# A two-group kernel with masked weights: results on another queue, masks among leaves, weight builds moved, a looser order

## The chip, the cores and the metric

The kernel runs on one core of a Trainium2 chip. The metric is the device time of one execution in microseconds (us). A core has TensorE (matrix products), VectorE and ScalarE (elementwise work), GpSimd, and SyncE, which here only issues transfers. Each engine runs its own instructions in one fixed order and waits where data, a buffer or a transfer isn't there yet. Transfers (DMAs) are issued by SyncE, ScalarE or GpSimd, and sixteen DMA engines carry them out.

## The reference

There are 8 batches of 256 tokens with 1024 features. The first layer adds, for each batch, a matrix product whose weights depend on the batch: a shared W0 plus a matrix of signs, +1 or -1 from a 0/1 mask of integers (1024 x 1024 per batch), scaled by the batch's coefficient. The second layer is a linear layer shared by all batches, plus a low-rank adapter (LoRA) of rank 16 picked for each batch.

```python
def _L0_cond_ref(hidden_states, W, b, coeff, mask):
    output = jnp.einsum('bsi,oi->bso', hidden_states, W) + b
    sign = (2 * mask - 1).astype(hidden_states.dtype)
    diff = jnp.einsum('bsi,bio->bso', hidden_states, sign)
    return output + diff * coeff[:, None, None]

def _L1_cond_ref(x, adapter_mapping, W, b, lora_As, lora_Bs):
    base_out = jnp.einsum('bti,oi->bto', x, W) + b
    A = lora_As[adapter_mapping]
    Bm = lora_Bs[adapter_mapping]
    lora_h = jnp.einsum('bti,bir->btr', x, A)
    lora_out = jnp.einsum('btr,bro->bto', lora_h, Bm)
    return base_out + lora_out * SCALING

x = x + _L0_cond_ref(x, L0_cond_W, L0_cond_b, condB_coeff, mask)
x = x + _L1_cond_ref(x, itok, L1_cond_W, L1_cond_b, lora_As, lora_Bs)
```

All data is float32, the masks are int32. A mask of one batch is 4 MB, all masks 32 MB.

## The kernel before, in words

**Two groups of four batches.** Each group runs the first layer of its four batches and then one second layer for all four: batches 0 to 3, second layer of group 0, batches 4 to 7, second layer of group 1. Everything is held transposed, features on the partitions.

**Pieces.** The effective weights of a batch are made in eight pieces of 128 x 1024 (`pieces`, lines 141 and 142); pieces 32 to 39 are those of batch 4. `load` (L173) issues a piece's mask (512 KB, L206), and for each of a batch's first four pieces also a tile of its tokens x (256 KB, L210), all on SyncE's queue. `build` (L222) turns the mask in place into weights in two steps: a conversion on ScalarE (L237, mask times 2c minus c) and an addition of W0 on VectorE (L245). The buffers of batch 4's first six pieces come from a pool of six ("w"), which the second layer of group 0 also uses for sums; the last two pieces, the second layer's results and the weight sums of batch 4 share a pool of ten ("q").

**First layer of batches 3 to 7 (`Seven`).** The 2 x 2 block product is done with seven products in place of eight (Strassen in Winograd's form). `operands` (L375) yields 20 steps a batch: eight pieces, the weight sums s1 to s4 in two halves each (L356, VectorE) and the token sums t1 to t4 (L373, VectorE). `products` (L447) issues seven products in 14 halves of 16 matmuls (L419). Results are read with the bias by ScalarE (`with_bias`, L438) or added by VectorE (`add`, L443). `Sevens.run_one` (L511) makes operands 10 steps ahead of the halves.

**Second layer (`second_layer`, L692).** Two levels of the same scheme. The outer level has seven products, `plan = ["A11", "A12", "S1", "S2", "S4", "S3", "A22"]`, run 0 to run 6. Each is again seven inner products of eight matmuls (L714) with seven weight tiles, the leaves a11, s1, s2, a12, s3, a22, s4 (256 KB each). The leaves are computed once, during group 0, and written to memory by GpSimd's queue (`keep`, L527, L531). `load_leaves` (L701, L704) reads the seven leaves of the next product into a pool of seven buffers, on SyncE's queue; it is called in the middle of each run (L815), so a leaf goes out when an older one has been used. `begin` (L762) starts the next product's a11 before the present product is finished. `read` (L766) takes results out of TensorE's banks: VectorE adds where there is something to add to, and ScalarE copies otherwise. `store` (L773) sends a finished 256 KB block of the output.

**What fills the second layer of group 0.** `next_masks(n)` (L871) issues loads of batch 4's first n pieces, and `next_weights(n)` (L877) makes the first n operand steps of batch 4 (their first four are the pieces 32 to 35). Both do nothing in group 1. A generator handed to `run` as `beside` gives a step at each of four places inside the run and what is left of it at its end. In the last run, `finish` (L830) gives the rest out between its last products.

**The order on the engines.** The tile framework plans each engine's order ahead, from the order in which the program names the instructions and from its own durations. `with behind(name)` (L144) adds an edge: the instructions in the block stand, on their own engine, after the instruction last kept under that name in `anchors`. So `behind("leaves")` puts masks after the last leaf issued, `behind("bias")` puts conversions after the last bias, `behind("adds")` puts additions of weights after the last sum, `behind("reads")` after the last read of the second layer.

Of the kernel before, what the change touches and what calls it, by code (L numbers as in the profile page):

```python
# [16 lines left out]
CG = 2  # L17
# [7 lines left out]
def kernel(  # L25
# [38 lines left out]
    nc = tc.nc  # L64
# [7 lines left out]
    NGROUP = B // GB  # L72
# [64 lines left out]
    anchors = {}  # L137
# [6 lines left out]
    def behind(what: str):  # L144
        return tc.issue_after(anchors[what].ins) if what in anchors else nullcontext()
# [104 lines left out]
    def load_to(n: int):  # L250
        nonlocal loaded
        while loaded < min(n, n_pieces):
            load(loaded)
            loaded += 1
# [5 lines left out]
    def bank(name):  # L260
        return psum.tile([P, 2, T], F32, tag="ps", name=name)
# [67 lines left out]
    class Seven:  # L329
# [105 lines left out]
        def with_bias(self, i, v, ps):  # L435
            for j in range(TPH):
                ot = i * TPH + j
                anchors["bias"] = nc.scalar.activation(  # L438
                    self.out(i, v)[:, j, :], ps[:, j, :], AF.Identity, bias=b0_sb[:, ot : ot + 1]
                )  # L440

        def add(self, i, v, ps):
            anchors["weights"] = anchors["adds"] = nc.vector.tensor_add(  # L443
                self.out(i, v), ps, self.out(i, v)
            )

        def products(self):  # L447

# [243 lines left out]
    def second_layer(group: int, y, first, first_steps, second):  # L692
# [6 lines left out]
        left_leaf, right = {}, {}  # L699

        def load_leaves(name):  # L701
            for n in ("a11", "s1", "s2", "a12", "s3", "a22", "s4"):
                t = lpool.tile([P, CG, OQ], F32, tag="l", name=f"l{group}_{name}_{n}")
                anchors["leaves"] = nc.sync.dma_start(t, leaf_at[name, n])  # L704
                left_leaf[name, n] = t
# [56 lines left out]
        def begin(n, name, r):  # L762
            banks[n] = bank(f"X_{group}_{n}")
            product(banks[n], left_leaf[name, "a11"], r.b[0, 0], first=True)

        def read(out, ps, other=None):  # L766
            if other is None:
                anchors["copies"] = nc.scalar.copy(out, ps)  # L768
                return anchors["copies"]
            own["reads"] = anchors["reads"] = nc.vector.tensor_add(out, ps, other)  # L770
            return anchors["reads"]

        def store(o, i, j, u, v, c=slice(0, CG), queue=nc.scalar):  # L773
            queue.dma_start(outT[GB * group + 2 * j + v, 2 * i + u][:, c], o)

        UV = [(0, 0), (0, 1), (1, 1), (1, 0)]
# [1 line left out]
        def run(n, name, r, seed, out, dest=None, beside=None, early=None, mid=None, late=None, then=None):  # L778

            leaf = {k: left_leaf.pop((name, k)) for k in ("a11", "s1", "s2", "a12", "s3", "a22", "s4")}
            other = seed or {uv: None for uv in UV}
            beside = beside or iter(())
            X = banks.pop(n)

            def done(uv):
                if dest:
                    store(out[uv], *dest, *uv)
                if then:  # L790
                    then(uv)

            read(out[0, 0], X, other[0, 0])
            Z = bank(f"Z_{group}_{n}")
            product(Z, leaf["s1"], r.t["t1"], first=True)
            if early:
                early()
            product(X, leaf["s2"], r.t["t2"])
            next(beside, None)
            read(out[0, 1], X, other[0, 1])  # L800
            Y = bank(f"Y_{group}_{n}")
            product(Y, leaf["a12"], r.b[1, 0], first=True)
            read(out[0, 0], Y, out[0, 0])
            done((0, 0))
            if mid:
                mid()
            if n + 1 == len(plan):
                finish(X, Z, leaf, r, other, out, dest, beside, done)
                return
            product(X, leaf["s3"], r.t["t3"])  # L810
            next(beside, None)
            read(out[1, 1], X, other[1, 1])
            read(out[1, 1], Z, out[1, 1])
            done((1, 1))
            load_leaves(plan[n + 1])  # L815
            begin(n + 1, plan[n + 1], right[plan[n + 1]])
            next(beside, None)
            product(X, leaf["a22"], r.t["t4"])
            read(out[1, 0], X, other[1, 0])
            done((1, 0))  # L820
            next(beside, None)
            if late:
                late()
            product(Z, leaf["s4"], r.b[1, 1])
            read(out[0, 1], Z, out[0, 1])
            done((0, 1))
            for _ in beside:
                pass

        def finish(X, Z, leaf, r, other, out, dest, beside, done):  # L830


            read(out[1, 1], Z, other[1, 1])
            product(X, leaf["s3"], r.t["t3"])
            next(beside, None)
            anchors["turn"] = read(out[1, 1], X, out[1, 1])
            done((1, 1))
            product(Z, leaf["s4"], r.b[1, 1])
            for _ in beside:
                pass  # L840
            read(out[0, 1], Z, out[0, 1])
            done((0, 1))
            product(X, leaf["a22"], r.t["t4"], by_tile=True)
            for c in range(CG):
                read(out[1, 0][:, c], X[:, c], other[1, 0][:, c])
                store(out[1, 0][:, c], *dest, 1, 0, c, (nc.sync, nc.scalar)[c])

        def quads(name):
            two = [pair(f"{name}{u}_{group}") for u in range(2)]
# [2 lines left out]
        def add(o, x):  # L852
            nc.vector.tensor_add(o, o, x)  # L853

        plan = ["A11", "A12", "S1", "S2", "S4", "S3", "A22"]
        right.update({"A11": first, "A12": second, "S4": Right(f"b22_{group}", b22)})
        big_t = {}

        def outer_sum(n, x, y, name):


            big_t[n] = [
                tpool.tile([P, TPH, T], F32, tag="T", name=f"T{n}_{group}_{v}") for v in range(2)
            ]
            right[name] = Right(f"T{n}_{group}", big_t[n])
            for v in range(2):
                nc.vector.tensor_sub(big_t[n][v], x[v], y[v])
                yield
            yield from right[name].sums()

        def next_masks(n):  # L871

            with behind("leaves"):
                if group + 1 < NGROUP:
                    load_to((group + 1) * GB * 2 * NG + n)

        def next_weights(n):  # L877
            if group + 1 < NGROUP:
                while sevens[group + 1].made < n:
                    sevens[group + 1].begin(sevens[group + 1].made + 1)  # L880
                    yield


        def ordered(steps):

            while True:
                with behind("reads" if "reads" in own else "layer"):
                    if next(steps, True):
                        return
                yield  # L890

        own = {}
        s3 = ordered(later["S3"] if group == 0 else iter(()))
# [3 lines left out]
        for _ in ordered(first_steps):  # L897
            pass
        t1 = ordered(outer_sum(1, b12, b11, "S1"))
        e1, c11, c12 = quads("e1"), quads("c11"), quads("c12")  # L900
# [3 lines left out]
            beside=chain(islice(s3, 1), ordered(second.sums()), islice(s3, 4), islice(t1, 2)),  # L904
            early=down,
            mid=lambda: up(0, 0, lower),
            late=lambda: up(0, 1, lower),
            then=lambda uv: add(c11[0, 0], e1[0, 0]) if uv == (1, 1) else None,
        )
        for uv in UV[1:]:  # L910
# [4 lines left out]
            dest=(0, 0),  # L915
            beside=chain(t1, s3, islice(t2, 2)),
        )
        next_masks(2)
        e5 = quads("e5")
        run(  # L920
            2, "S1", right["S1"], None, e5,
            beside=chain(t2, ordered(right["S4"].sums())),
            then=lambda uv: add(c12[uv], e5[uv]),
        )
        next_masks(4)
        run(
            3, "S2", right["S2"], e1, e1,
            beside=chain(ordered(outer_sum(3, b22, b12, "S3")), next_weights(2)),
            then=lambda uv: add(c12[uv], e1[uv]),
        )  # L930
        c21, c22 = quads("c21"), quads("c22")
# [1 line left out]
        run(  # L933
            4, "S4", right["S4"], c12, c12,
            dest=(0, 1),
            beside=chain(ordered(outer_sum(4, b21, big_t[2], "A22")), next_weights(3)),
            mid=lambda: up(1, 0, upper),
            late=lambda: up(1, 1, upper),
        )
# [1 line left out]
        def add_e5():  # L941

            for uv in UV:
                with behind("reads"):
                    add(c22[uv], e5[uv])
                yield

        run(5, "S3", right["S3"], e1, e1, beside=chain(add_e5(), next_weights(4)), then=lambda uv: add(c21[uv], e1[uv]))


        next_masks(6)
# [1 line left out]
        def last_quarter():  # L953
            for u, v in UV:
                add(c22[u, v], e1[u, v])
                store(c22[u, v], 1, 1, u, v)
                yield

        run(6, "A22", right["A22"], c21, c21, dest=(1, 0), beside=last_quarter())
        nonlocal limit  # L960
        limit = n_pieces

# [143 lines left out]
```

## Time and profile before

| | before |
|---|---|
| time, median of 3 runs | 418.19 us (417.73 to 419.43) |
| the profiled execution's own time | 420.21 us |
| its span, first to last instruction | 418.5 us |
| TensorE busy | 404.1 us (97%), 2554 matmuls, mean granted clock 0.992 |
| VectorE busy | 312.8 us (75%) |
| ScalarE busy | 136.4 us (33%) |
| GpSimd busy | 42.8 us (10%) |
| moved by DMA | 99.56 MB, 238 GB/s on average |

The stages of the span, read from TensorE's timeline: batches 0 to 3 until about 114.7 us, second layer of group 0 from 114.7 to 219.4, batches 4 to 7 from 219.4 to 320.8, second layer of group 1 from there to the end. Inside the first of the second layers, the runs begin their a11 at about 114.7 (A11), 128.4 (A12), 140.1 (S1), 159.5 (S2), 174.3 (S4), 190.5 (S3) and 203.9 us (A22).

How to read the lines: L714 is line 714 of the kernel; "X<-T,l_S_a" names what an instruction writes and reads, without buffer numbers; a note in brackets at the end of a line is the time that the engine stood idle before it and what ended it. PE is TensorE, PEld its weight load, DVE VectorE, ACT ScalarE, POOL GpSimd, SPq SyncE's queue. In tables of stretches the columns are the stretch, its length, the busy time (and number) of TensorE, its weight loads, VectorE, ScalarE and GpSimd, then TensorE's granted clock, the busy share of the DMA engines and GB/s. In tables of waits, the numbers are the time in all, how often, and the longest.

### The profile page before, as it was taken

How to read it: one execution, taken by the hardware profiler on the slowest of the kernel's cores; microseconds unless marked ns; L12 is line 12 of the kernel's file. 1: busy time of each engine (PE TensorE's matmuls, PEld its weight loads, DVE VectorE, ACT ScalarE, POOL GpSimd, SP SyncE). 2: the span in 40 equal slices, each digit the busy share in tenths (PEclk: the TensorE clock that was granted, in tenths of full speed). 3: DMA queues.
4: the chain of work that ended last, by engine and by line, in shares of the span. 5: the costliest groups of instructions: out<-in, count | busy, mean ns of one | idle time of the engine just before them, and what ended most of it. 6: DMA issues, size and time to landing. Idle time of an engine off the chain costs nothing.

```text
span 418.5 us, 6751 instructions
## 1 busy us (share of the span) xinstructions
PE 404.1 (97%) x2554; PEld 359.8 (86%) x2554; DVE 312.8 (75%) x446; ACT 136.4 (33%) x221; POOL 42.8 (10%) x85
## 2 busy tenths in 40 slices
PE   8999999999999977899999999999999999999996
PEld 6888888899968766678889999999999788888885
DVE  3357688999706883997899999899843177898593
ACT  4443625771034012303041844537421330101100
POOL 0000252009750120000000001300000000000000
PEclk9999999999999996999999999999999999999999
DMA  8999999961996795745699965904011337554644
GB/s 291 404 401 398 401 408 413 402 248 41 364 366 215 233 330 222 257 161 167 199 369 360 407 210 191 311 3 152 27 52 60 93 125 232 171 153 157 217 153 151
DMA packets 42404, 99.56 MB, mean 238 GB/s; under 512 B 5636, under 2 KB 6404, under 8 KB 42372
## 3 DMA queue, kind: packets, MB, share of 16 engines
q1 hardware_dynamic: 32690, 76.17, 52.0%
q0 software_dynamic: 4928, 14.71, 9.4%
q10 hardware_dynamic: 4754, 8.26, 5.4%
q8 instruction: 20, 0.33, 0.3%
q14 instruction: 12, 0.10, 0.1%
HBM read 79.19 MB, written 19.92 MB: 237 GB/s over the span
## 4 chain that ended last, share of the span: by engine, by line
PE 84%; DMA 9%; DVE 4%; SPq 1%; issue 1%; DVEq 0%
PE X L714 22%; PE X L419 15%; PE ps L278 13%; PE Z L714 10%; PE Z L419 8%; PE Y L714 5%; PE ps L303 4%; DMA l_S_a<-leaf_S_a 4%; PE Y L419 3%; PE G L732 2%; DMA x<-xT 2%; PE psh L749 2%; DMA w_sb<-w0T 2%; DVE w L245 1%; DMA w<-mask 1%; DMA l_S_s<-leaf_S_s 1%
## 5 line engine op out<-in xcount | busy, mean ns | idle before, releaser
L245 DVE TENSOR_TENSOR w<-w,w_sb 128x1024 f32<-128x1024 f32 (+1 forms) x67 | 77.4, 1172 | 27.3 <-ACT w L237 20.8
L237 ACT ACTIVATE w<-w,neg_c,two_c 128x1024 f32<-128x1024 int32 (+1 forms) x67 | 78.6, 1204 | 57.6 <-DMA w<-mask 46.9
L278 PE MATMUL ps<-x,w 128*128 128x256 f32 x256 | 55.4, 379 | 0.0
L278 PEld LDWEIGHTS ps<-x,w 128*128 128x128 f32 x256 | 48.6, 190 | 6.6
L853 DVE TENSOR_TENSOR c<-c,e 128x512 f32<-128x512 f32 x48 | 32.1, 683 | 11.3 <-ACT e L768 6.7
L438 ACT ACTIVATE y<-X,b_sb 128x128 f32<-128x128 f32 x60 | 17.1, 368 | 67.1 <-PE X L419 67.1
L419 PE MATMUL X<-t,s 128*128 128x128 f32 x288 | 34.1, 275 | 0.7 <-DVE s L356 0.7
L419 PEld LDWEIGHTS X<-t,s 128*128 128x128 f32 x288 | 33.0, 192 | 0.9 <-DVE s L356 0.9
L742 ACT COPY c<-G 128x512 f32<-128x512 f32 x32 | 16.5, 599 | 48.4 <-PE G L732 47.4
L303 PE MATMUL ps<-x,w 128*128 128x256 f32 x128 | 28.5, 384 | 0.3 <-DVE w L245 0.3
L303 PEld LDWEIGHTS ps<-x,w 128*128 128x128 f32 x128 | 24.6, 193 | 4.3 <-DVE w L245 0.9
L768 ACT COPY e<-X 128x512 f32<-128x512 f32 x16 | 9.4, 586 | 56.3 <-PE X L714 56.3
L770 DVE TENSOR_TENSOR e<-Y,e 128x512 f32<-128x512 f32 x8 | 5.5, 689 | 25.8 <-PE Y L714 14.0
L714 PE MATMUL X<-T_t,l_S_s 128*128 128x256 f32 x96 | 22.8, 380 | 1.0 <-DVE e L770 1.0
L770 DVE TENSOR_TENSOR c<-X,c 128x512 f32<-128x512 f32 (+1 forms) x26 | 16.6, 645 | 8.7 <-PE X L714 8.7
L419 PE MATMUL X<-t,w 128*128 128x128 f32 x192 | 22.5, 276 | 0.1
L419 PEld LDWEIGHTS X<-t,w 128*128 128x128 f32 x192 | 21.9, 192 | 0.3 <-DVE y L443 0.3
L356 DVE TENSOR_TENSOR s<-w,w 128x1024 f32<-128x1024 f32 x18 | 21.7, 1217 | 0.1
L714 PEld LDWEIGHTS X<-T_t,l_S_s 128*128 128x128 f32 x96 | 18.2, 190 | 3.9 <-DVE e L770 1.4
L419 PE MATMUL Z<-t,s 128*128 128x128 f32 x160 | 18.8, 275 | 0.0
L419 PE MATMUL Y<-x,w 128*128 128x128 f32 x160 | 18.7, 275 | 0.0
L419 PE MATMUL X<-x,w 128*128 128x128 f32 x160 | 18.7, 275 | 0.0
(144 smaller groups left out, 664.7 us busy)
## 6 DMA issues: line engine op xcount, KB each, us to landing
w<-mask SPq DMA_DIRECT2D x61, 512.0 KB, 7.1
l_S_s<-leaf_S_s SPq DMA_DIRECT2D x32, 256.0 KB, 2.7
x<-xT SPq DMA_DIRECT2D x31, 256.0 KB, 7.2
outT<-c ACTq DMA_DIRECT2D x30, 256.0 KB, 2.6
l_A_s<-leaf_A_s SPq DMA_DIRECT2D x24, 256.0 KB, 2.7
l_S_a<-leaf_S_a SPq DMA_DIRECT2D x24, 256.0 KB, 2.6
w<-w1T SPq DMA_DIRECT2D x16, 256.0 KB, 7.2
leaf_A_s<-A_s POOLq DMA_DIRECT2D x12, 256.0 KB, 6.6
```

The source lines that it names most:

```text
L237: nc.scalar.activation(w[:, i], m[:, i], AF.Identity, bias=neg_c[:, b : b + 1], scale=two_c[:, b : b + 1],)
L245: weff_at[k] = nc.vector.tensor_add(w[:, i], w[:, i], w0_of(k)[:, i])
L278: nc.tensor.matmul(ps[j // 2][:, j % 2, :], lhsT=w[:, c, j * P : (j + 1) * P], rhs=x_sb[b, g][:, c, :],  start=first and j % 2 == 0, stop= ...
L303: nc.tensor.matmul(ps[ot // 2][:, ot % 2, :], lhsT=w[:, h, j * P : (j + 1) * P], rhs=x_sb[0, c // CG][:, c % CG, :], start=c == 0 and ot % ...
L356: anchors["weights"] = op(s, self.w[x, a], self.w[y, a])
L419: anchors["products"] = nc.tensor.matmul(ps[:, j, :], lhsT=w[:, c, j * P : (j + 1) * P], rhs=r, start=first and a == 0 and c == 0 and j == ...
L438: anchors["bias"] = nc.scalar.activation(self.out(i, v)[:, j, :], ps[:, j, :], AF.Identity, bias=b0_sb[:, ot : ot + 1])
L714: anchors["inner"] = nc.tensor.matmul(ps[:, j, :], lhsT=l[:, c, j * P : (j + 1) * P], rhs=r[:, c, :], start=first and c == 0 and j == 0, s ...
L742: nc.scalar.copy(dest[b // 2][u, b % 2], ps[b])
L768: anchors["copies"] = nc.scalar.copy(out, ps)
L770: own["reads"] = anchors["reads"] = nc.vector.tensor_add(out, ps, other)
L853: nc.vector.tensor_add(o, o, x)
```

## The change

Four edits, all of them in how work is ordered or queued; what is computed stays.

- *Stores.* In group 0 all results go out on GpSimd's queue; before, ScalarE issued them, and SyncE one half of the last block. In group 1 the queues are as before.
- *Masks.* `next_masks(2)` and `next_masks(4)` ahead of runs 2 and 3 are gone. In their place `load_leaves` lets one more mask (with its x) out between the leaves a12 and s3, from product S1 on: piece 32 with S1, 33 with S2, 34 with S4, 35 with S3, 36 with A22. `next_masks(6)` ahead of run 6 stays.
- *Builds.* Operand steps 1 and 2 of batch 4 were made in run 3, step 3 in run 4, step 4 in run 5. Now steps 1 and 2 are made in run 5, and 3 and 4 in run 6.
- *Order.* The last bias of a batch, (1, 0), is no longer kept under "bias", and the sum (0, 1) no longer under "adds", so later conversions and additions needn't stand behind them.

```diff
         def with_bias(self, i, v, ps):
             for j in range(TPH):
                 ot = i * TPH + j
-                anchors["bias"] = nc.scalar.activation(
+                sent = nc.scalar.activation(
                     self.out(i, v)[:, j, :], ps[:, j, :], AF.Identity, bias=b0_sb[:, ot : ot + 1]
                 )
+            if (i, v) != (1, 0):
+                anchors["bias"] = sent
 
         def add(self, i, v, ps):
-            anchors["weights"] = anchors["adds"] = nc.vector.tensor_add(
-                self.out(i, v), ps, self.out(i, v)
-            )
+            anchors["weights"] = nc.vector.tensor_add(self.out(i, v), ps, self.out(i, v))
+            if i == v:
+                anchors["adds"] = anchors["weights"]
...
         def load_leaves(name):
             for n in ("a11", "s1", "s2", "a12", "s3", "a22", "s4"):
+                if n == "s3":
+                    next_masks(max(0, plan.index(name) - 1))
                 t = lpool.tile([P, CG, OQ], F32, tag="l", name=f"l{group}_{name}_{n}")
...
-        def store(o, i, j, u, v, c=slice(0, CG), queue=nc.scalar):
+        out_queues = (nc.gpsimd, nc.gpsimd) if group + 1 < NGROUP else (nc.scalar, nc.sync)
+
+        def store(o, i, j, u, v, c=slice(0, CG), queue=out_queues[0]):
             queue.dma_start(outT[GB * group + 2 * j + v, 2 * i + u][:, c], o)
...
-                store(out[1, 0][:, c], *dest, 1, 0, c, (nc.sync, nc.scalar)[c])
+                store(out[1, 0][:, c], *dest, 1, 0, c, out_queues[1 - c])
...
-        next_masks(2)
         e5 = quads("e5")
...
-        next_masks(4)
         run(
             3, "S2", right["S2"], e1, e1,
-            beside=chain(ordered(outer_sum(3, b22, b12, "S3")), next_weights(2)),
+            beside=ordered(outer_sum(3, b22, b12, "S3")),
...
         run(
             4, "S4", right["S4"], c12, c12,
             dest=(0, 1),
-            beside=chain(ordered(outer_sum(4, b21, big_t[2], "A22")), next_weights(3)),
+            beside=ordered(outer_sum(4, b21, big_t[2], "A22")),
...
-        run(5, "S3", right["S3"], e1, e1, beside=chain(add_e5(), next_weights(4)), then=lambda uv: add(c21[uv], e1[uv]))
+        run(5, "S3", right["S3"], e1, e1, beside=chain(add_e5(), next_weights(2)), then=lambda uv: add(c21[uv], e1[uv]))
...
-        run(6, "A22", right["A22"], c21, c21, dest=(1, 0), beside=last_quarter())
+        run(
+            6, "A22", right["A22"], c21, c21,
+            dest=(1, 0),
+            beside=chain(last_quarter(), next_weights(4)),
+        )
```

## The prediction

> **What bounds the kernel now.** I read the page's first two parts, the waits of TensorE, its timeline from 110 to 300 us, the SyncE queue and the chain of waits in the same stretch, and last the busy time of VectorE by stretches. TensorE is busy for 404.1 of 418.5 us; it starts at about 17 us, and nothing before 140 us is touched by the change. So what can be won is what TensorE loses later. Its waits, longest first, and its timeline in the first second layer:
>
> ```profile
> PE X L714 <- DMA l_S_a<-leaf_S_a: 5.4, 2, 4.7
> ```
>
> ```profile
> 152.96 1.89 PE L714 MATMUL X<-T_t,l_S_s 128*128 128x256 f32 x8
> 159.51 3.75 PE L714 MATMUL X<-T,l_S_a 128*128 128x256 f32 x8 [4.66 <-DMA l_S_a<-leaf_S_a]
> 163.06 2.23 PE L714 MATMUL X<-T_t,l_S_a 128*128 128x256 f32 x8
> 165.12 1.89 PE L714 MATMUL Z<-T,l_S_s 128*128 128x256 f32 x8
> ...
> 171.49 1.99 PE L714 MATMUL X<-T_t,l_S_s 128*128 128x256 f32 x8 [1.03 <-DVE e L770]
> 174.27 1.96 PE L714 MATMUL X<-y,l_S_a 128*128 128x256 f32 x8 [0.79 <-DMA l_S_a<-leaf_S_a]
> ...
> 188.67 1.99 PE L714 MATMUL X<-b_t,l_S_s 128*128 128x256 f32 x8 [1.00 <-DVE c L770]
> ```
>
> The reader sees one large hole and three small ones. The large one costs more than its 4.66 us: the eight matmuls after it take 163.06 - 159.51 = 3.55 us and the next eight 2.06, where eight take 1.73 elsewhere, so another 1.82 + 0.33 = 2.15 us. The holes' sum from 154 to 189 us is 4.66 + 2.15 + 1.03 + 0.79 + 1.00 = 9.63 us. Two more lie outside (0.38 at 142.3, 0.71 at 279.6). Why the leaf is late stands in SyncE's queue:
>
> ```profile
> 146.06 0.32 SPq L704 DMA_DIRECT2D l_S_s<-leaf_S_s  x1
> 146.49 0.37 SPq L206 DMA_DIRECT2D w<-mask  x1
> 146.91 0.42 SPq L210 DMA_DIRECT2D x<-xT  x1
> 147.43 0.37 SPq L206 DMA_DIRECT2D w<-mask  x1
> 147.86 0.74 SPq L210 DMA_DIRECT2D x<-xT  x1
> 150.12 0.33 SPq L704 DMA_DIRECT2D l_S_a<-leaf_S_a  x1
> ```
>
> ```profile
> 150.12 9.26 DMA l_S_a<-leaf_S_a
> ```
>
> Two masks and two x tiles, 2 x (512 + 256) KB = 1.5 MB, go out just ahead of leaf a11 of S2, which then takes 9.26 us to land where the median of such leaves is 2.6. The leaf itself leaves late too: the buffer that it takes is free at about 147.9, when the product with A12's a22 is done (it starts at 145.95, the next product at 147.78), but SyncE stands in the masks until 148.6 and then waits 1.5 us for an earlier leaf's landing. Further on it waits for output stores, 3.1 us before 153.63. Those stores are ScalarE's; I read this as a shared count of transfers in flight, since no data links the two. The next three leaves come out between 153.6 and 156.5 for that reason, but they aren't needed until 160 or later.
>
> VectorE is the second bound, and only from about 203 us on:
>
> ```profile
> 203.00:216.00 13.00, 13.00 (x62) 11.45 (x61) 12.94 (x23) 2.48 (x2) 0.00 (x0) 1.00 0.81 275
> 216.00:228.60 12.60, 12.60 (x100) 12.19 (x99) 12.60 (x19) 3.51 (x6) 0.00 (x0) 1.00 1.01 373
> ```
>
> ```profile
> 185.67 2.35 DVE L245 TENSOR_TENSOR w<-w,w_sb 128x1024 f32<-128x1024 f32 x2
> 187.94 0.68 DVE L770 TENSOR_TENSOR c<-X,c 128x512 f32<-128x512 f32 x1
> ...
> 227.45 1.21 DVE L356 TENSOR_TENSOR s<-s,w 128x1024 f32<-128x1024 f32 x1
> ```
>
> ```profile
> 228.78 1.43 PE L419 MATMUL X<-t,s 128*128 128x128 f32 x11
> ```
>
> (Third column of the stretches after the two of TensorE: VectorE's busy time, 12.94 of 13.00 and 12.60 of 12.60.) The second half of batch 4's s2 starts at 227.45 and ends at about 228.6, and TensorE takes it at 228.8: VectorE has almost no lead there. And the pair of builds at 185.67 stands ahead of the read at 187.94 that TensorE waits for at 188.67.
>
> **What the Trainium skill says.** "TensorE: Matmul & The Clock Gate", section "Part 1: The HAM clock gate", says that about 3.4 us without work brings the clock to half; the trace agrees (4.66 us idle, then 3.55 us for 1.73 us of work, clock 0.52 in the stretch 158 to 164), while holes of 1 us cost nothing after them. "DMA: Bandwidth & Descriptors", section "SWDGE vs HWDGE vs iDMA", says that GpSimd's transfers feed other internal queues of the same DMA engines, served in turn: so the stores still share bandwidth with leaves after the change. "SBUF — State Buffer", section "Who interferes with whom", says that VectorE's two-input tensor_tensor has no mode that shuts GpSimd out of writing descriptors. The trace agrees: GpSimd's issues at 151 to 156 us took 0.54 us each beside a VectorE that was busy throughout.
>
> **The change part by part.**
>
> *Masks.* Mask 32 with its x goes out between leaves a12 and s3 of S1 (at about 140.6), 33 inside S2's (about 153.7), 34 in S4's, 35 in S3's, 36 in A22's, 37 after. Leaf a11 of S2 then has no mask in front; eight transfers back in SyncE's queue is a leaf landed long before. It can go at about 148.1, and even at 3.6 us is there at 152, before 154.85, when TensorE asks. Hole and half clock go: -4.66 - 2.15 = -6.81. Leaf a11 of S4 likewise, issued at about 160 against a need at about 166: -0.79. Late next are leaves s3, a22, s4 behind each mask, issued at 155 to 158.5 and needed at 168 to 173; covered by about 10 us. The mask needs a free w buffer at 140; at 146.49 it had waited 0.2 us only.
>
> *Stores.* 16 issues leave ScalarE and SyncE for GpSimd, 16 x 0.54 = 8.6 us on an engine that is idle after 156. GpSimd's own queue holds S3's leaf stores (151 to 156), needed after 178 only, and the adapters' loads, which wait until 259. SyncE loses its waits for stores (4.5 us among leaves, 6.2 us from 207 to 230, all among transfers with slack). A store on GpSimd may land later: its transfers have medians from 3.9 to 7.6 us, against 2.6 for ScalarE's; the last buffers (c21, c22) are issued by about 222 and the sums s4 that could want them start at 231.5. Zero, with up to +2 us if VectorE waits.
>
> *Builds.* The additions of pieces 32 and 33 leave the end of run 3 (S2): the read at 187.94 comes 2.27 us earlier, TensorE's 1.00 us goes: -1.00. They return at the end of run 5, tied behind its last read (209.55); 34 (now at 198.97) and 35 (210.15) go to run 6, behind the read at 216.30. So between 203 and 228.6 there were builds 35 to 39, and there will be 32 to 39: three more at 1.13 us (pairs take 2.27 between starts), 3.4 us in a stretch where VectorE has 0.06 us free. What was hidden in the holes of VectorE before 203 (0.24, 1.71, 0.43 and 1.03 us) loses that cover. TensorE has about 0.3 us of lead at s2, so it waits 3.1 us: about 0.6 before X of s3 in run 6, the rest at the two halves of s2. Bounds: 0 (two-step token sums, 1.3 us, and last-quarter additions, 4 x 0.6 us, slide into earlier holes or behind) to 3.4 + 2.15 (one hole long enough to halve the clock). I take +3.1: the sum of work is fixed, only its order is open.
>
> *ScalarE's order.* Conversions need no longer stand behind the last bias of a batch, nor additions of VectorE behind the sum of (0, 1). ScalarE is idle for most of 230 to 310, VectorE waited for it 0.80 and 1.18 us at 287 and 298, with TensorE unharmed. 0; bounds -0.7 (the hole at 279.6) to +1.
>
> The hole of 1.03 at 171.49 stays: it is VectorE's order (four sums of b_t before the read), and that work is unchanged; laid out by hand from 158.6 the read ends 1.1 us late again.
>
> Sum: -6.81 - 0.79 - 1.00 + 3.1 = -5.5. Against the profiled execution, 420.21 (span 418.5 and 1.7 around it), that is 414.7; the median of the runs shown is 2.0 lower, 418.19, so 412.7.
>
> **Rivals.**
> (a) Leaves on time, and VectorE's extra builds find cover. For it: 5 us of VectorE idle from 188 to 203 once the earlier builds are gone. Against: the builds are written behind later reads. Then -8.6: 409.6.
> (b) The leaf is still late, because bandwidth and not order holds it: the same bytes move between 140 and 160, in stretches of 0.86 to 1.01 DMA share. Half of the 6.81 stays, and VectorE's price is paid: -5.5 + 3.4 = -2.1: 416.1. Against: only 0.75 MB of masks moves with S2, and 0.46 to 0.74 share at 134 to 146 has room for the other.
> (c) Slower: a mask inside the set blocks its leaves. If no w buffer is free at 140, mask 32 waits on SyncE for S3's leaf stores (issued by 156, median 5.9 to landing), and s3 of S1 behind it comes at about 164.5 instead of before 152.96: 11.5 us of hole and 2.2 of half clock in place of 6.81, so +6.9; with -1.8 and +3.1 the total is +8.2: 426.4. It decides as soon as the wait passes about 5.5 us beyond need. For it: only six w buffers, two held by S3. Against: the wait of 0.2 at 146.49, and the four others were last used before 125.
>
> **How the numbers follow.** Forecast (-5.5) 0.52, (a) 0.24, (b) 0.14, (c) 0.10. The forecast's own spread is -3 to -7. No change within 0.5%, 2.1 us, is about what this measurement can tell. Faster by more: 0.52 + 0.24 and half of (b), 0.83 less some doubt, 0.81; slower 0.11, same 0.08. Range 408.5 to 417.5: (a) with a little more at the bottom, (b) with 1.4 more at the top.
>
> **What would show it.** TensorE's wait for l_S_a of 4.7 us gone, and the stretch 158 to 164 at full clock; no wait of 1.0 at run 4's third product. Batch 4 starts about 8 us earlier than 219.4, and then TensorE waits about 2.5 us for DVE s (line 356) in its third product. Wrong if the leaf of S2 lands after TensorE's need, if a leaf of S1 waits behind mask 32, or if batch 4 runs without a wait for s.

## The result, and the profile after

| | before | after |
|---|---|---|
| median | 418.19 us (417.73 to 419.43) | 412.55 us (411.92 to 414.21) |
| the profiled execution's own time | 420.21 us | 411.92 us |
| its span | 418.5 us | 410.3 us |
| TensorE's mean granted clock | 0.992 | 1.000 |
| first second layer, from TensorE's timeline | 114.73 to 219.40: 104.67 us | 114.85 to 210.98: 96.13 us |
| batches 4 to 7 | 219.40 to 320.84: 101.44 us | 210.98 to 312.93: 101.95 us |
| from there to the end | 97.66 us | 97.37 us |

The ratio is 0.9861, 95% interval 0.9833 to 0.9888: 5.8 us faster, between 4.7 and 7.0. The forecast was 412.7. But the two columns differ by 5.6 us in the medians and by 8.3 us in the profiled executions, and the forecast's 5.5 was summed from a profiled one. So it needs explaining how the forecast came so near.

TensorE's timeline after the change, where the large hole was, and at the start of batch 4:

```profile
154.81 1.89 PE L718 MATMUL X<-T,l_S_a 128*128 128x256 f32 x8
...
161.81 1.89 PE L718 MATMUL Y<-T,l_S_a 128*128 128x256 f32 x8
165.10 1.53 PE L718 MATMUL X<-y,l_S_a 128*128 128x256 f32 x6 [1.39 <-DMA l_S_a<-leaf_S_a]
166.47 1.89 PE L718 MATMUL X<-T_t,l_S_s 128*128 128x256 f32 x8
...
180.25 1.99 PE L718 MATMUL X<-b_t,l_S_s 128*128 128x256 f32 x8
...
214.55 3.74 PE L419 MATMUL Y<-x,w 128*128 128x128 f32 x32
218.58 2.02 PE L419 MATMUL Z<-t,s 128*128 128x128 f32 x16 [0.29 <-DVE s L356]
220.85 2.02 PE L419 MATMUL X<-t,s 128*128 128x128 f32 x16 [0.25 <-DVE s L356]
...
226.78 3.84 PE L419 MATMUL X<-t,s 128*128 128x128 f32 x32 [0.34 <-ACT y L438]
```

Leaf a11 of S2 is there when TensorE asks for it (154.81, no bracket), the clock stays full, and run 4's third product starts at 180.25 without a wait. What is left in this layer is 1.39 us for S4's a11, and in batch 4 three waits of 0.29, 0.25 and 0.34 us. The lines at 218.58 and 220.85 are the surprise: after Y, TensorE takes Z (s1 x t1) first and then X (s2 x t2). In the kernel before it took s2 first. SyncE's queue shows when the leaf left:

```profile
148.10 0.32 SPq L708 DMA_DIRECT2D l_S_a<-leaf_S_a  x1
...
153.28 0.32 SPq L708 DMA_DIRECT2D l_S_a<-leaf_S_a  x1
153.70 0.42 SPq L206 DMA_DIRECT2D w<-mask  x1
154.17 0.42 SPq L210 DMA_DIRECT2D x<-xT  x1
155.01 0.33 SPq L708 DMA_DIRECT2D l_S_s<-leaf_S_s  x1
```

The a11 of S2 leaves at 148.10, two microseconds sooner than before and with no mask in front, and lands after 3.5 us in place of 9.26; mask 33 stands between a12 (153.28) and s3 (155.01).

### The profile page after: what moved, and what is told of

Read it like the earlier page. It is cut to its first block, busy times and chain, and to the rows that moved or that the text cites. A ratio compares the mean times of both kernels' runs of the same rounds, so it can differ in the third digit from the quotient of the medians.

```text
span 410.3 us, 6785 instructions
## 1 busy us (share of the span) xinstructions
PE 401.6 (98%) x2554; PEld 358.1 (87%) x2554; DVE 312.2 (76%) x446; ACT 136.3 (33%) x221; POOL 52.0 (13%) x102
## 3 DMA queue, kind: packets, MB, share of 16 engines
q0 software_dynamic: 6224, 18.90, 12.3%
## 4 chain that ended last, share of the span: by engine, by line
PE 90%; DMA 4%; DVE 3%; issue 1%; SPq 1%; ACT 0%; DVEq 0%
PE X L718 24%; PE X L419 17%; PE ps L278 13%; PE Z L718 11%; PE Z L419 8%; PE Y L718 5%; PE ps L303 4%; PE Y L419 3%; PE G L736 2%; PE psh L753 2%; DMA w_sb<-w0T 2%; DVE w L245 1%; DMA w<-mask 1%; DMA l_S_a<-leaf_S_a 1%; SPq L197 1%
## 5 line engine op out<-in xcount | busy, mean ns | idle before, releaser
L419 PEld LDWEIGHTS Z<-t,s 128*128 128x128 f32 x160 | 18.4, 192 | 0.5 <-PE Y L419 0.5
```

Of the source, the lines that this page charges most:

```text
L419: anchors["products"] = nc.tensor.matmul(ps[:, j, :], lhsT=w[:, c, j * P : (j + 1) * P], rhs=r, start=first and a == 0 and c == 0 and j == ...
```

## The experiments

The working theory was this: the gain is the queue ahead of S2's a11 (masks), the stores and the looser order do nothing, and the builds leave VectorE in debt in batch 4 as the prediction has it, but the planner's new order of products on TensorE pays most of it. The rivals stand in each expectation. Ratios are against the kernel before on the same chip: e1 to e4, e5 to e8 and e9 to e12 ran on three chips, where the kernel before had medians of 418.70, 417.89 and 418.71 us.

| run | median us | ratio to before (95%) |
|---|---|---|
| e1 masks only | 414.91 | 0.9906 (0.9878 to 0.9935) |
| e2 stores only | 418.70 | 1.0003 (0.9973 to 1.0032) |
| e3 builds only | 419.25 | 1.0029 (0.9999 to 1.0060) |
| e4 order only | 418.41 | 0.9984 (0.9956 to 1.0012) |
| e5 all four, again | 412.13 | 0.9850 (0.9814 to 0.9887) |
| e6 all four, s2 first in batch 4 | 415.08 | 0.9924 (0.9902 to 0.9947) |
| e7 all but builds | 413.08 | 0.9889 (0.9851 to 0.9928) |
| e8 all four and two more moves | 408.99 | 0.9781 (0.9747 to 0.9815) |
| e9 all four, no mask among S2's leaves | 410.47 | 0.9797 (0.9771 to 0.9823) |
| e10 all four, builds earlier | 410.53 | 0.9799 (0.9773 to 0.9825) |
| e11 all but stores | 412.46 | 0.9845 (0.9819 to 0.9871) |
| e12 all but order | 411.65 | 0.9835 (0.9808 to 0.9863) |

### Each edit alone

e1 is the kernel before with the edit to `load_leaves` and without the two `next_masks` lines:

```diff
             for n in ("a11", "s1", "s2", "a12", "s3", "a22", "s4"):
+                if n == "s3":
+                    next_masks(max(0, plan.index(name) - 1))
...
-        next_masks(2)
...
-        next_masks(4)
```

> The kernel before with the masks alone put among the leaves. Theory Q (the late leaf is a matter of what stands ahead of it in SyncE's queue): the hole of 4.66 us ahead of S2's a11 goes although ScalarE still sends the stores; 4 to 7 us faster than before (4.66, 0.79 of S4's a11, and 2.15 of half clock where a run has it). Rival B (bandwidth and the stores' share of it hold the leaf): the leaf still lands after 154.85, half of the hole stays, 1 to 3 us faster.

e2 changes `store`'s queues alone, e3 the four `beside` arguments alone, e4 `with_bias` and `add` alone, each as in the change's diff.

> The kernel before with the stores of group 0 alone on GpSimd's queue. Theory Q: masks still stand ahead of S2's a11, so only SyncE's wait of 1.5 us before it goes; 0 to 2 us faster. Rival B: the stores' share was what held the leaf; 3 to 6 us faster. A rival in which stores on GpSimd release buffers late: slower, with waits of VectorE for DMA in batch 4.

> The kernel before with the four builds alone moved to runs 5 and 6. As predicted: -1.0 us (the read in run 4) and +3.1 us (s2 of batch 4 late), so 2 us slower than before. Rival N (TensorE's new order of products in batch 4, s1 ahead of s2, hides the late s2): between 1.0 us faster and 0.5 slower, and waits for s of at most 1 us in all.

> The kernel before with the looser order alone. As predicted 0, bounds 0.7 us faster to 1 us slower; TensorE's wait of 0.71 us at 279.6 may go. Rival: conversions stand ahead of biases and hold them up; over 1 us slower.

Masks alone win 3.9 us (2.7 to 5.1), just under theory Q's 4 to 7. The waits in e1's timeline show why it isn't more:

```profile
165.21 1.53 PE L716 MATMUL X<-y,l_S_a 128*128 128x256 f32 x6 [1.54 <-DMA l_S_a<-leaf_S_a]
182.64 2.90 PE L716 MATMUL X<-b_t,l_S_s 128*128 128x256 f32 x8 [2.30 <-DVE c L772]
275.99 2.05 PE L419 MATMUL X<-t,s 128*128 128x128 f32 x16 [1.40 <-DVE s L356]
```

The hole of 4.66 us is gone with the stores still on ScalarE, so rival B falls. But two waits for VectorE are longer than in the profile before: the read of run 4 with 2.30 us for 1.00, the s2 of batch 6 with 1.40 for 0.71. For the first, e1's VectorE timeline has the pair of builds ahead of the read; the large hole had given VectorE time to catch up:

```profile
179.63 2.35 DVE L245 TENSOR_TENSOR w<-w,w_sb 128x1024 f32<-128x1024 f32 x2
181.90 0.68 DVE L772 TENSOR_TENSOR c<-X,c 128x512 f32<-128x512 f32 x1
```

For the second the cause is not shown: e2 and e4, which leave masks and builds alone, don't have that wait at all.

e2: no difference, within 1.3 us. Its hole is 4.20 us in place of 4.66: theory Q, and no sign of late buffers. It also separates two causes that the prediction names together, a leaf that leaves late and a leaf that stands behind masks. In e2 the a11 of S2 leaves almost as early as in the changed kernel, but behind the two masks:

```profile
148.31 0.60 SPq L704 DMA_DIRECT2D l_S_a<-leaf_S_a  x1
```

It lands 10.5 us later, where it takes 5.0 us in e1 and 3.5 in the changed kernel. The DMA engines moved about as much in both, by the rates of 146 to 154 us an estimated 2.4 MB in e2 and 2.5 MB after the change. So it is what stands ahead of the leaf that makes it late, not the time at which it leaves and not a lower rate of the DMA engines.

e4: no difference that can be told, within 1.8 us. The hole of 0.71 isn't in e4's profile, but it isn't in e2's either, so it is no proof for the looser order.

e3: between no change and 2.5 us slower, so the time alone decides neither for the prediction's 2 us nor against it. The trace does. Its holes before batch 4 include one of 3.97 us, with 2.84 us lost to slow matmuls after it, as in a kernel whose masks were left alone; in batch 4 it waits for s only twice:

```profile
226.47 2.02 PE L419 MATMUL Z<-t,s 128*128 128x128 f32 x16 [0.29 <-DVE s L356]
228.74 2.02 PE L419 MATMUL X<-t,s 128*128 128x128 f32 x16 [0.25 <-DVE s L356]
```

That is 0.54 us of waiting, and Z ahead of X. So the new order on TensorE comes with the builds alone. Batches 4 to 7 take 101.95 us here and 100.45 in e2 and in e4: by the timelines the moved builds cost 1.50 us in them, and they win the 1.00 us of the read in run 4, which is gone.

### Where VectorE's debt went

TensorE's order in batch 4 of the kernel before, for comparison with the lines above (X<-t,s is s2 x t2, Z<-t,s is s1 x t1):

```profile
226.55 1.95 PE L419 MATMUL X<-t,s 128*128 128x128 f32 x16
228.33 0.61 PE L419 MATMUL Z<-t,s 128*128 128x128 f32 x4
228.78 1.99 PE L419 MATMUL X<-t,s 128*128 128x128 f32 x16
230.61 3.29 PE L419 MATMUL Z<-t,s 128*128 128x128 f32 x28
```

The planner orders by its own estimates, which are not on record. That it puts s1 x t1 first because it expects s2 later is argued, not shown; that the order follows the builds is shown by e3 and, below, by e7. e6 is the changed kernel with that taken back:

```diff
+                with behind("s2") if self.b == GB and left == "s1" else nullcontext():
+                    for j in range(TPH):
+                        anchors["products"] = nc.tensor.matmul(
...
+            if left == "s2":
+                anchors["s2"] = anchors["products"]
```

> The changed kernel once more, on one chip with the runs sent beside it. Every theory: the ratio of the result again, 0.983 to 0.989, and a profile with a wait of about 1.4 us for S4's a11 and waits of under 1 us in all in batch 4.

> The changed kernel, but in batch 4 the 32 matmuls of s1 x t1 are tied behind those of s2 x t2, as they stood in the kernel before. Theory N (TensorE's new order covers a late s2; VectorE's sum was right): TensorE waits 2.5 to 3.5 us for s of batch 4, and the kernel is 1.5 to 2.7 us slower than the changed one. Rival V (VectorE has no such debt): the same time as the changed kernel within 0.5 us, waits for s under 1 us.

e6's timeline of TensorE:

```profile
217.04 3.74 PE L420 MATMUL Y<-x,w 128*128 128x128 f32 x32
223.34 2.02 PE L420 MATMUL X<-t,s 128*128 128x128 f32 x16 [2.56 <-DVE s L356]
225.85 2.05 PE L420 MATMUL X<-t,s 128*128 128x128 f32 x16 [0.49 <-DVE s L356]
```

2.56 + 0.49 = 3.05 us of waiting, where the prediction had 3.1. VectorE was busy without a break there (13.00 of 13.00 us from 212 to 225). Theory N holds and rival V falls: VectorE's debt was as large as computed. It is TensorE that doesn't stand still for it. The median is 415.08 - 412.13 = 2.95 us above e5's, a little more than the 1.5 to 2.7 expected. The timelines give 2.0 us of it to the order: batches 4 to 7 take 103.96 us in e6 and 101.94 in e5. The rest isn't assigned.

e7 puts the builds back where they were, in the changed kernel:

> The changed kernel with the four builds where they were before (runs 3, 4 and 5). As predicted: the builds' move costs 2.1 us on balance, so this one is about 2 us faster than the changed one. Theory M (once the leaves come on time, VectorE falls behind in run 3, and the pair of builds there costs more than the 1.0 us of before): a wait of about 2.3 us for the read of run 4, a total 1 to 2.5 us slower than the changed one.

```profile
182.59 1.99 PE L718 MATMUL X<-b_t,l_S_s 128*128 128x256 f32 x8 [2.30 <-DVE c L774]
```

The read of run 4 is late by 2.30 us, as in e1, and batch 4 runs without a wait, with s2 first again. The median is 0.95 us above e5's, with intervals that overlap, so neither size nor sign is sure from the times; the 2 us faster of the prediction is not what they show. The timelines agree with the median: e7 reaches batch 4 2.2 us later than e5 (213.32 and 211.12), and takes 100.45 us for batches 4 to 7 in place of 101.94, so 1.5 less, 0.7 us slower on balance. The same move of the builds costs the same 1.5 us as in e3, but it wins 2.2 us in run 4 instead of 1.0. The parts alone (-3.9, 0, +1.2, -0.7 us) come to -3.4, the whole to -5.8. A wait that the masks open and the builds close would explain 1.3 us of that difference; the rest is within the intervals.

e11 and e12 take the stores' edit and the order's edit out of the changed kernel:

> The changed kernel with the stores of group 0 back on ScalarE's queue. As predicted: the same within 1 us. Rival (SyncE's waits for stores are what made leaves late): a leaf late again in S2 or S4, 1.5 us slower or more.

> The changed kernel with the old, tighter order (last bias and sum (0, 1) kept under their names). As predicted: the same within 1 us, at most a wait of 0.7 us for s in batch 6 back.

Both are as fast as the changed kernel: ratios of 0.9845 and 0.9835 against 0.9850 for e5. Neither edit does anything that these runs can tell.

### What was left on the table

The changed kernel still waits for S4's a11 (1.1 to 1.5 us) and for s in batch 4. Two moves go at these:

```diff
-                    next_masks(max(0, plan.index(name) - 1))
+                    next_masks(max(0, plan.index(name) - 1 - (plan.index(name) > 2)))
...
-            beside=ordered(outer_sum(4, b21, big_t[2], "A22")),
+            beside=chain(ordered(outer_sum(4, b21, big_t[2], "A22")), next_weights(2)),
...
-        run(5, "S3", ..., beside=chain(add_e5(), next_weights(2)), ...)
+        run(5, "S3", ..., beside=chain(add_e5(), next_weights(3)), ...)
```

> The changed kernel with no mask among S2's leaves (32 with S1, 33 with S4, 34 with S3, 35 with A22) and the first two builds at the end of run 4, where VectorE has holes, one in run 5 and one in run 6. If the wait for S4's a11 comes of mask 33, and the waits in batch 4 of builds that stand too late: both go, 1.5 to 2.3 us faster than the changed kernel. If S3's leaf stores hold that leaf: its wait stays, and at most 0.9 us is won.

> The changed kernel with only the first of e8's two moves: no mask among S2's leaves. If mask 33 and its x hold S4's a11: its wait of 1.1 to 1.9 us goes, 1 to 1.5 us faster than the changed kernel, with the waits of batch 4 (0.9 us in all) as they were. If S3's leaf stores hold it: no difference.

> The changed kernel with only the second of e8's moves: builds 32 and 33 at the end of run 4, 34 in run 5, 35 in run 6. If VectorE's debt is what makes batch 4 wait: those 0.9 us go, 0.5 to 1 us faster than the changed kernel, with S4's a11 late as it was. If the debt comes of something else: no difference.

In e9 the wait for S4's a11 is gone, and that of batch 4 stays (0.29, 0.25 and 0.34 us); in e10 it is the other way round (1.46 us for the leaf, none in batch 4). So mask 33 held that leaf, not S3's leaf stores, which e9 has too; and late builds made batch 4 wait. Whether the leaf was held by its place behind the mask or by busy DMA engines isn't separated here: their busy share from 158 to 164 us was 0.97 after the change and 0.76 in e9. e9 and e10 are 2.0 and 1.9 us below e11 and 1.2 and 1.1 below e12, on the same chip; 1 to 1.5 and 0.5 to 1 were expected. e8 has both moves. Its TensorE waits, in full, are

```profile
PE idle_ps L100 <- DVE h_sb L95: 1.4, 1, 1.4
PE Z L718 <- issue: 0.4, 1, 0.4
```

and its VectorE timeline at the end of run 4 shows the two builds in what was a hole of 1.56 us, with the next read late by nothing that TensorE noticed:

```profile
189.03 2.36 DVE L245 TENSOR_TENSOR w<-w,w_sb 128x1024 f32<-128x1024 f32 x2
191.30 0.69 DVE L774 TENSOR_TENSOR e<-X,e 128x512 f32<-128x512 f32 x1
```

At 408.99 us it is the fastest of all: 3.1 us below e5, more than the 1.5 to 2.3 expected. On the timelines, batch 4 starts at 209.47 instead of 211.12, and batches 4 to 7 take 100.53 us instead of 101.94. The named waits that went are 1.10 and 0.88 us. The rest, about 1.1 us, lies partly ahead of anything that was moved (e8 begins S1's a11 at 140.14, e5 at 140.61) and partly around the three waits of batch 4, which cost 1.4 us from start to start although their names account for 0.88.

## Why the prediction was right, and where it was right by luck

*The late leaf: right.* It said -6.81 for S2's a11, issued at about 148.1, with mask 33 at about 153.7. The trace has 148.10 and 153.70, no hole and full clock, and e1 shows that the masks alone do it. Of the two reasons that it gave for the lateness, the masks ahead count and the late issue doesn't (e2).

*S4's a11 and the read at 171.49: wrong in where, near in sum.* The prediction let 0.79 go and 1.03 stay. After the change TensorE asks for S4's a11 ahead of s2 (at 163.7 instead of 166), finds it 1.39 us late, and has the read in time. 1.82 us became 1.39: -0.43 where -0.79 was said. This new order is in e1 too, so it comes with the masks. The prediction expected the leaf well ahead of its need at 166; it took 4.7 us from 160.28, and e9 shows that mask 33 makes it late.

*The read of run 4: right.* -1.00, and nothing waits at 180.25. What it missed is that with the leaves on time this wait would have been 2.30 us, so the edit is worth more than the profile of before could show (e7).

The first second layer was thus predicted at -8.6 and measured at -8.54 us, between the two profiled executions.

*The builds: the step that failed.* "TensorE has about 0.3 us of lead at s2, so it waits 3.1 us" took TensorE's order of products as given. VectorE's side was right to the tenth: s2's second half ends at 223.3, 12.3 us after batch 4's start, where it was 228.6 - 219.4 = 9.2, so 3.1 later. But s1 x t1 doesn't need s2, is 3.57 us of work, and was moved ahead. In the trace the waits are 0.29 + 0.25 + 0.34 = 0.88 us, and from start to start the price is 1.5 us (e7 and e3). So the term was mis-sized by 1.6 us; with the old order, e6, the waits are 3.05 us. The sign that it named, about 2.5 us of waiting for s in batch 4, came as 0.54. Batches 4 to 7 take only 0.51 us more than in the profile before because that one lost about 1 us at batch 6's s2, which the profiles of e2, e4 and e7 don't.

*Why the total agreed all the same.* The prediction put its sum on the profiled execution, 420.21, and moved to the median by a constant 2.0 us. But that execution was a long one: of 54 runs of the kernel before beside e1 to e4 (415.5 to 422.96 us), 44 were shorter. The profiles of e2 and e4, which leave the masks alone and have a time like that of before, had no hole at s2 of batch 6, e4 none for S4's a11 (0.79), and 1.7 us of slow matmuls in place of 2.15. So the profiled kernel before had more to win than its median execution: 8.3 us between the profiles, 5.6 between the medians, of which difference 2.0 lies before the change and 0.6 after it. The sum of -5.5 was 2.8 us too small for the profiles, 1.6 of it the builds and about 1 the hole of batch 6, and the distance of the profiles from the medians, 2.6, made up for that. The stage before batch 4 was good; the landing on 412.55 was part luck.

*The rivals.* (a), cover for the builds, came true in part, and by another way than described there: not free time on VectorE but other work for TensorE, and 0.88 us of waits stayed. Its -8.6 from the profiled 420.21 gives 411.6, where the profiled execution after took 411.92. (b), bandwidth, falls with e1, and with e2, where the leaf leaves early and lands late behind the masks. (c), a mask that blocks its own set's leaves, didn't come: mask 32 went out at 140.79 and s3 of S1 at 142.12.

*Stores and order.* Priced at 0 each, and no difference from 0 can be told, in both directions (e2 and e11, e4 and e12). SyncE's waits for output stores among the leaves, 4.5 us before, are gone in e2, which takes as long as before, so they had slack. They are gone in e1 and e11 too, where ScalarE sends the stores, so the queue of the stores alone doesn't make them. Stores don't land later from GpSimd: the median is 5.1 us, from ScalarE it was 5.5. The Trainium skill says in "SBUF — State Buffer", section "Who interferes with whom", that VectorE's tensor_tensor has no mode that locks GpSimd out, and that it takes only the read side of the ports that the two share, where writing descriptors needs the write side; the page marks this last step as inferred. The trace agrees: the store issues (17, where the prediction counted 16) took 0.54 us each, while VectorE was busy for 87% of 143 to 214 us.

## What to carry to other kernels

Look first at what stands ahead of a late transfer in its own queue: one mask at a time, placed where the next needed tile is several products away, was worth 3.9 us where the change of the stores' queue was worth nothing that can be told, and one mask put in the wrong set still cost 1.1 to 1.6 us. Where an engine's work is moved, work out the debt, but don't charge it to the other engine before asking what else that engine could do meanwhile, since a planner may find it, as it did here. And take the baseline from many executions: here, in a kernel with holes, one profiled execution stood 2 us off the median. An edit's worth depends on what else has changed: by the timelines the builds' move loses 0.5 us with late leaves and wins 0.7 us with leaves on time.

## What the runs showed of the hardware

Some holes cost more than their length, and others of the same length don't. The table gives the extra time of the two products after a hole, from the starts in the timelines (eight matmuls of the second layer normally take 1.73 us, the first six of them 1.30, and sixteen of batch 4 1.79):

| hole, us | run | extra after it, us |
|---|---|---|
| 4.66 | before | 1.82 + 0.33 |
| 4.73 | e4 | 1.72 |
| 4.20 | e2 | 1.00 + 0.76 |
| 3.97 | e3 | 1.82 + 1.02 |
| 2.56 | e6, batch 4 | none |
| 2.30 | e7, run 4 | none |
| 2.30 | e1, run 4 | 0.97 + 0.81 |
| 1.89 | e6, S4's a11 | 0.35 (six matmuls) + 1.40 |

"TensorE: Matmul & The Clock Gate", section "Part 1: The HAM clock gate", of the Trainium skill has about 3.4 us without work before the clock halves. The holes of 4 us agree. Those of 1.89 in e6 and 2.30 in e1 do not: they were followed by slow matmuls at a lower clock, while the same 2.30 in e7 wasn't. e1's stretch after its hole shows it (columns as before, the clock, 0.64, is the third from the right); in e6 the clock was 0.60 from 168 to 171 us:

```profile
182.60:186.00 3.40, 3.36 (x10) 2.77 (x11) 2.13 (x3) 1.24 (x1) 0.00 (x0) 0.64 0.40 153
```

The measurement decides: of four holes between 1.89 and 2.56 us here, two cost another 1.8 us and two cost nothing more. What decides between them isn't shown.

Whole executions spread likewise: the kernel before, with its large hole, ran in 415.5 to 422.96 us (54 runs), while e8, without one, stayed within 408.89 to 409.03 (6 runs). The record has the mean clock of each execution. Of those 54, the 25 with a clock of at most 0.994 have a median of 419.5 us, the four with at least 0.999 one of 416.0; clock and time correlate at -0.68, so the clock goes with about half of the spread (-0.68 squared is 0.47). The rest isn't explained, and no run changed the clock by itself.
